# Four-layer image kernel: spectral row transforms moved between the input blocks, a wider layer norm in the attention, and the triangle layer's two outer stages written in 512-column steps

## The chip, the cores and the metric

The kernel runs on one core of one Trainium2 chip. The metric is device time in microseconds (us) for one launch, as the median of several runs. All arithmetic is in float32.

## The reference, cut to what matters

The input `x` has shape 1 x 256 x 256 x 128: 65,536 pixels of 128 channels. Four layers follow, each of the form `x = x + layer(group_norm(x))`.

```python
# layer 0: attention along each image row, 4 heads of 32
zn = layer_norm(z) * ln_scale + ln_bias
q, k, v, g = zn @ Wq, zn @ Wk, zn @ Wv, sigmoid(zn @ Wg)
bias = zn @ Wb                                   # 4 numbers a pixel
o = softmax(q k^T / sqrt(32) + bias) v;  out = (g * o) @ Wo

# layer 1: a recurrence of 16 steps whose coefficients are spectra of 7x7 kernels
A_f = fft2(pad(A_real + 1j * A_imag, 256, 256))  # the same for B
...

# layer 2: triangle
pn = layer_norm(pair)
left, right = sigmoid(pn @ g_in) * (pn @ p_in)   # two halves of 128
out = einsum('bikd,bjkd->bijd', left, right / 256)
out = layer_norm(out) @ p_out
out = sigmoid(pn @ g_out) * out

# layer 3: 3x3 convolution, then a 128 x 128 product
```

The 2-D transforms of the 7 x 7 kernels are computed as two small products: first over the rows (the "spectral row transforms" of the change), later over the columns.

## The kernel before, in words

Activations live in device memory in transposed form, channels on the 128 partitions and pixels along the free axis. `run` calls the stages one after another, and each stage writes an image of 32 MiB that the next one reads.

- `transpose_in` (L137 to L160) reads 64 blocks of 1024 pixels. A block is loaded on SyncE's queue (L146), transposed by eight 128 x 128 TensorE transposes into a PSUM tile `pt` of two banks (L150, pool `p0s` with three buffers), copied out half by VectorE and half by ScalarE (L154, L156), put through two `bn_stats` (L159), and stored to `xT` on GpSimd's queue (L160).
- `spectra` (L532) does the row transforms after that. For each of the two kernels A and B it clears a tile `ka`, fills it with four small loads on SyncE's queue (L545), and for 16 groups of four channels does four matmuls `ph` (L56, 21 rows contracted, 14 output rows, 256 columns) and one strided copy into `H`: on VectorE for A (L555), on ScalarE for B (L553). Each finished half of `H` is stored to `HD`.
- `attention` first sums up the statistics (`group_affine`, the aggregation at L75), makes the weights, and runs a front stage over 64 blocks of 1024 pixels, in two halves of 512. A half calls `layer_norm` (L105 to L118): matmul `zc`, Square on ScalarE to `sq`, matmul `var`, Ln and Exp on ScalarE to `rs`, one VectorE operation to `zn` (L118). Then comes the matmul `pbias` with four output rows, and a VectorE addition to `bi` (L212). `zn` and `bi` are stored on GpSimd's queue (L213, L214). Afterwards `attend_bounded` does the attention, in an order pinned by hand.
- `recurrence` follows, over 64 blocks.
- `triangle` has three stages over the same pixels. The first (L830 to L887) works on 64 blocks of 1024 columns, in an order pinned by hand. For block b it does the three sigmoid gates (`pe`, `pgl`, `pgr`) and the two gated products (`pl`, `pr`), and between them the centring, squares, variance and normalising of block b + 2. Every matmul pair covers 1024 columns, and ScalarE, VectorE operations are 1024 wide. Two table loads of ScalarE stand in each block (L832), around Ln and Exp. The output gates of the first 22 blocks stay in on-chip memory (`kept`); those of the other 42 go through `gateD`. The second stage (L908 to L928) multiplies left and right for each of 128 channels. The third (L940 to L965) takes blocks of 1024 columns: matmuls `zc`, `var`, `py`, in between Square, Ln, Exp on ScalarE and `on`, `y`, `x3`, `bn_stats` on VectorE.
- `convolution` is the last stage.

Where no order is pinned, a scheduler at build time fixes one order for each engine. Every engine then works through its own list in that order and waits, at an instruction, for what that instruction needs; a tile pool with n buffers lets n uses of a tile be under way. In the front stage of the attention and in `transpose_in` the order is the scheduler's; Ln, Exp and table loads are chained in the order of the text (`chain`).

Of the kernel before, what the change touches and what calls it, by code (L numbers as in the profile page):

```python
# [9 lines left out]
F32 = mybir.dt.float32  # L10
# [7 lines left out]
P = 128  # L18
# [12 lines left out]
class Kernel:  # L31
# [105 lines left out]
    def transpose_in(self, xT, stats):  # L137

        nc, tc = self.nc, self.tc
        x = self.i["x"].rearrange("b h w c -> (b h w) c")  # L140
        with ExitStack() as c:
            io = c.enter_context(tc.tile_pool(name="p0", bufs=3))
            ps = c.enter_context(tc.tile_pool(name="p0s", bufs=3, space=PSUM))
            for b in range(NPIX // 1024):
# [15 lines left out]
                nc.gpsimd.dma_start(xT[:, b * 1024:(b + 1) * 1024], xf)  # L160

    def attention(self, xT, x1T, znT, biasD, stats0, stats1):
        nc, tc, I = self.nc, self.tc, self.i
        with ExitStack() as c:
# [31 lines left out]

            with ExitStack() as c1:
                io = c1.enter_context(tc.tile_pool(name="a1", bufs=3))
                work = c1.enter_context(tc.tile_pool(name="a1w", bufs=3))
                ps = c1.enter_context(tc.tile_pool(name="a1s", bufs=2, space=PSUM))  # L200
                self.table(LN_EXP)
                for b in range(NPIX // 1024):
                    xin = io.tile([P, 1024], F32, name="xin")
                    nc.sync.dma_start(xin, xT[:, b * 1024:(b + 1) * 1024])
                    zn = io.tile([P, 1024], F32, name="zn")
                    bi = io.tile([NH, 1024], F32, name="bi")
                    for h in range(2):
                        s = slice(h * 512, (h + 1) * 512)
                        self.layer_norm(zn[:, s], xin[:, s], lc, cb, work, ps, "table")
                        pb = ps.tile([NH, 512], F32, name="pbias")  # L210
                        self.mm(pb, w["b"], zn[:, s])
                        nc.vector.tensor_scalar_add(bi[:, s], pb, wb["b"])  # L212
                    nc.gpsimd.dma_start(znT[:, b * 1024:(b + 1) * 1024], zn)  # L213
                    nc.gpsimd.dma_start(biasD[:, b * 1024:(b + 1) * 1024], bi)  # L214
# [317 lines left out]
    def spectra(self, HD_, name):  # L532

        nc, tc, I = self.nc, self.tc, self.i
        with ExitStack() as c:
            sp = c.enter_context(tc.tile_pool(name=name, bufs=1))
            ps = c.enter_context(tc.tile_pool(name=name + "s", bufs=2, space=PSUM))
            tu = self.load(sp, I["c_rows"], "tu")
            H = sp.tile([46, N, HC], F32, name="H")
            for n, (re, im) in enumerate((("A_real", "A_imag"), ("B_real", "B_imag"))):  # L540
                kr, ki = (I["L1_conv_" + x].rearrange("c p q -> p c q") for x in (re, im))
                ka = sp.tile([3 * KS, HC, 2 * KS], F32, name=f"ka{n}")
                nc.vector.memset(ka, 0.0)
                for p0, q0, src in ((0, 0, kr), (0, KS, ki), (KS, 0, ki), (2 * KS, KS, kr)):
                    nc.sync.dma_start(ka[p0:p0 + KS, :, q0:q0 + KS], src)  # L545
                o = 32 * n
                for c0 in range(0, HC, 4):
                    ph = ps.tile([P, 4, N], F32, name="ph", tag=f"ph{n}")
                    for cc in range(4):
                        self.mm(ph[o:o + 2 * KS, cc, :], ka[:, c0 + cc, :], tu)  # L550
                    dst = H[o:o + 2 * KS, :, c0:c0 + 4].rearrange("q u c -> q c u")
                    if n:
                        nc.scalar.copy(dst, ph[o:o + 2 * KS])  # L553
                    else:
                        nc.vector.tensor_copy(dst, ph[o:o + 2 * KS])  # L555
                nc.sync.dma_start(HD_[n], H[o:o + 2 * KS])

# [240 lines left out]
    def triangle(self, x2T, x3T, leftD, rightD, gateD, prodD, stats2, stats3):  # L798
        nc, tc, I = self.nc, self.tc, self.i
        with ExitStack() as c:  # L800
            wp = c.enter_context(tc.tile_pool(name="tw", bufs=1))
            w, wb = {}, {}
            with tc.tile_pool(name="twp", bufs=2, space=PSUM) as ps0:
# [8 lines left out]
                for nm, m, c0, sc, bb in (("pl", "p", 0, lnw, lnb), ("pr", "p", P, lnw, lnb),  # L812
                                        ("gl", "g", 0, lnw, lnb), ("gr", "g", P, lnw, lnb),
                                        ("e", "e", 0, lnw, lnb), ("o", "o", 0, low, lob)):
                    rw = raw[m][:, c0:c0 + P]
                    pb = ps0.tile([P, 2], F32, name="tpb" + nm, tag="gn")
                    self.mm(pb[:, 0:1], rw, bb)
                    wb[nm] = wp.tile([P, 1], F32, name="twb" + nm)
                    nc.vector.tensor_copy(wb[nm], pb[:, 0:1])
                    w[nm] = wp.tile([P, P], F32, name="tw" + nm)  # L820
                    nc.vector.tensor_scalar_mul(w[nm], rw, sc)


            NB, KEPT = NPIX // 1024, 22
            kept = c.enter_context(tc.tile_pool(name="tk", bufs=1)).tile([P, KEPT, 1024], F32, name="kept")
            with ExitStack() as c1:
                io = c1.enter_context(tc.tile_pool(name="t1", bufs=2))
                work = c1.enter_context(tc.tile_pool(name="t1w", bufs=2))
                ps = c1.enter_context(tc.tile_pool(name="t1s", bufs=3, space=PSUM))
                pin = lambda f: lambda *a, **k: tc.keep_in_program_order(f(*a, **k))  # L830
                mm, act, stt = pin(self.mm), pin(self.act), pin(nc.vector.scalar_tensor_tensor)
                table = lambda n: tc.keep_in_program_order(nc.scalar.preload_act_table_set(n))  # L832
                D = [{} for _ in range(NB)]
                flat = lambda t: t.rearrange("p k n -> p (k n)")

                def product(name, wt, src, **kw):
                    z = ps.tile([P, 2, 512], F32, name=name, **kw)
                    for k in range(2):
                        mm(z[:, k], wt, src[:, k * 512:(k + 1) * 512])
                    return flat(z)  # L840

                def centre(b):
                    if b < NB:
                        xin = io.tile([P, 1024], F32, name="xin")
                        nc.sync.dma_start(xin, x2T[:, b * 1024:(b + 1) * 1024])
                        D[b]["zc"] = product("zc", lc, xin, bufs=1)

                def squares(b):
                    if b < NB:
                        sq = D[b]["sq"] = work.tile([P, 1024], F32, name="sq")  # L850
                        act(sq, D[b]["zc"], AF.Square, bias=cb)

                def variance(b):
                    if b < NB:
                        D[b]["var"] = product("var", self.omat, D[b]["sq"], tag="z")

                def normalise(b):
                    if b < NB:
                        rs = work.tile([P, 1024], F32, name="rs")
                        act(rs, D[b]["var"], AF.Ln, bias=self.eps)  # L860
                        act(rs, rs, AF.Exp, scale=-0.5)
                        zn = D[b]["zn"] = work.tile([P, 1024], F32, name="zn", bufs=3)
                        stt(zn, D[b]["zc"], cb, rs, ALU.add, ALU.mult)

                def gate(b, nm, out):
                    z = product("p" + nm, w[nm], D[b]["zn"], tag="z")
                    act(out, z, AF.Sigmoid, bias=wb[nm])
                    return out

                def gated(b, nm, g, dst):  # L870
                    z = product("p" + nm, w["p" + nm], D[b]["zn"], tag="z")
                    o = io.tile([P, 1024], F32, name="t" + nm)
                    stt(o, z, wb["p" + nm], g, ALU.add, ALU.mult)
                    nc.gpsimd.dma_start(dst[:, b * 1024:(b + 1) * 1024], o)

                table(LN_EXP)
                for b in range(2):
                    centre(b)
                    squares(b)
                    variance(b)  # L880
                    normalise(b)
                table(SIGMOID)
                for b in range(NB):
                    e = kept[:, b] if b < KEPT else io.tile([P, 1024], F32, name="te")
                    gate(b, "e", e)
                    if b >= KEPT:
                        nc.gpsimd.dma_start(gateD[:, b * 1024:(b + 1) * 1024], e)  # L887
                    gl = gate(b, "gl", work.tile([P, 1024], F32, name="sgl"))
                    centre(b + 2)
                    squares(b + 2)  # L890
# [40 lines left out]
            with ExitStack() as c1:  # L931
# [5 lines left out]
                for b in range(NB):  # L937
# [12 lines left out]
                    for k in range(2):  # L950
                        self.mm(zc[:, k], self.cmat, pr[:, k * 512:(k + 1) * 512])
# [249 lines left out]
```

## Time and profile before

| What | us |
|---|---|
| median of three runs | 6563.59 (6561.63 to 6569.74) |
| profiled execution, its own time | 6569.74 |
| its span, first to last instruction | 6567.7 |
| input transposes, to the last `bn_stats` | 0 to 199 |
| spectral row transforms, to the aggregation | 199 to 329 |
| front stage of the attention, with its weights | 329 to 844 |
| attention | 844 to 2293 |
| recurrence | 2293 to 4378 |
| triangle, weights and first stage | 4378 to 5170 |
| triangle, second stage | 5170 to 5560 |
| triangle, third stage | 5560 to 5973 |
| convolution | 5973 to 6568 |

Over the span TensorE is busy 92%, VectorE 63%, ScalarE 57%. The stage limits are read from the first and last instructions of each stage. The profile gives matmuls as instructions: a float32 matmul of the program is two of them, so `pe` with 128 matmuls of 512 columns shows 256. Since matmuls overlap in their pipeline, the duration of one (592 ns for 512 columns) is longer than the distance between two starts; where the text counts TensorE time it uses the distance.

### The profile page before, as it was taken

To read this page: it belongs to the slowest core of one execution; us is meant where nothing else is said; L and a number is where in the kernel's file an instruction comes from. 1 tells how busy PE (TensorE), PEld (TensorE's weight loads), DVE (VectorE), ACT (ScalarE), POOL (GpSimd) and SP (SyncE) were. 2 spreads that over 40 slices of the span, in tenths; PEclk is the share of its full clock that TensorE was granted. 3 is DMA by queue.
4 is the path that set the end of the run, shared out by engine and by line. 5 is a ranking of instruction groups with operands and counts; after the bars stand their busy time and mean duration, and the time that the engine had idled before them with its cause. 6 is when DMAs were issued, how large, how long until landed. Compare 5 with 4: busy or idle time off the path is not lost. (4 is left out here: it accounts for less than half of the span.)

```text
span 6567.7 us, 72931 instructions
## 1 busy us (share of the span) xinstructions
PE 6011.7 (92%) x27637; PEld 2686.6 (41%) x27637; DVE 4161.4 (63%) x5400; ACT 3756.5 (57%) x4945; POOL 367.5 (6%) x720
## 2 busy tenths in 40 slices
PE   5778889999999989999999999979999999887999
PEld 4211145555555423333333333324444587333554
DVE  5333357777777767887878878763333222778775
ACT  1245556666666666666666666657777543444332
POOL 1011100000000000000000000000111111000000
PEclk6599989999999989999999999999999999998999
DMA  9333322222222121111111111113444688895331
GB/s 339 85 135 136 136 76 69 78 69 76 71 74 73 60 60 49 52 49 49 49 49 56 49 49 52 49 48 131 156 174 176 210 271 261 270 336 207 131 134 64
DMA packets 276107, 765.35 MB, mean 117 GB/s; under 512 B 46148, under 2 KB 82265, under 8 KB 273681
## 3 DMA queue, kind: packets, MB, share of 16 engines
q1 hardware_dynamic: 192908, 469.11, 23.4%
q0 software_dynamic: 82848, 291.55, 11.3%
q8 instruction: 222, 3.64, 0.2%
q14 instruction: 129, 1.05, 0.1%
HBM read 433.63 MB, written 326.89 MB: 116 GB/s over the span
## 5 line engine op out<-in xcount | busy, mean ns | idle before, releaser
L327 DVE TENSOR_TENSOR e<-sc,bT 128x1024 f32<-128x1024 f32 x512 | 624.4, 1220 | 159.5 <-PE sc L56 159.5
L50 ACT ACTIVATE e<-e 128x1024 f32<-128x1024 f32 x512 | 538.3, 1051 | 146.2 <-DVE e L327 146.0
L56 PE MATMUL m<-v,U 128*128 128x512 f32 x1152 | 517.5, 595 | 23.3 <-DVE v L1059 23.3
L56 PE MATMUL var<-sq,omat 128*128 128x512 f32 x768 | 388.0, 614 | 140.4 <-ACT sq L50 139.2
L50 ACT ACTIVATE rs<-var,eps 128x512 f32<-128x512 f32 (+1 forms) x256 | 230.6, 901 | 365.9 <-PE var L56 257.5
L50 ACT ACTIVATE dn<-dn 128x256 f32<-128x256 f32 (+1 forms) x640 | 290.3, 454 | 154.0 <-DVE dn L327 145.7
L56 PE MATMUL sc<-tq,tk 32*128 32x256 f32 x4096 | 321.0, 400 | 2.7 <-DVE e L327 2.7
L830 DVE SCALAR_TENSOR_TENSOR tl<-pl,twbpl,sgl 128x1024 f32<-128x1024 f32 x64 | 82.2, 1284 | 359.7 <-ACT sgr L50 336.9
L56 PEld LDWEIGHTS m<-v,U 128*128 128x128 f32 x1152 | 210.4, 191 | 241.5 <-issue 234.3
L212 DVE TENSOR_SCALAR bi<-pbias,wbb 4x512 f32<-4x512 f32 x128 | 94.5, 738 | 316.1 <-PE pbias L56 316.1
L56 PEld LDWEIGHTS var<-sq,omat 128*128 128x128 f32 x768 | 132.7, 189 | 382.1 <-ACT sq L50 273.4
L919 DVE COPY k<-pt 128x256 f32<-128x256 f32 x256 | 96.8, 419 | 285.0 <-PE pt L913 277.0
L56 PE MATMUL nd<-e,tv 128*32 128x256 f32 x4096 | 274.9, 386 | 0.0
L56 PE MATMUL zc<-xin,lc 128*128 128x512 f32 x512 | 269.2, 629 | 4.7 <-DVE zn L830 3.8
L56 PE MATMUL nd<-e,ones 128*32 128x256 f32 x4096 | 268.2, 379 | 0.0
L56 PE MATMUL po<-k,k 128*128 128x256 f32 x1024 | 253.2, 390 | 8.2 <-DVE k L919 0.6
L56 PEld LDWEIGHTS sc<-tq,tk 32*128 32x128 f32 x4096 | 213.9, 184 | 111.8 <-issue 103.7
L56 PE MATMUL zi<-xf,gwi 128*64 128x512 f32 x512 | 188.5, 613 | 67.9 <-DVE q L615 67.9
L50 ACT ACTIVATE sq<-zc,cb 128x512 f32<-128x512 f32 (+1 forms) x192 | 159.3, 829 | 136.8 <-PE zc L56 136.8
L56 PE MATMUL za<-ev,hs 14*128 14x512 f32 x256 | 156.9, 720 | 84.9 <-DVE A L611 79.1
L1079 ACT COPY o<-pt 128x512 f32<-128x512 f32 x128 | 74.6, 584 | 273.4 <-PE pt L1077 263.0
L50 ACT ACTIVATE rs<-rs 128x512 f32<-128x512 f32 (+1 forms) x256 | 216.1, 844 | 7.2
(343 smaller groups left out, 12363.4 us busy)
## 6 DMA issues: line engine op xcount, KB each, us to landing
xin<-x2T SPq DMA_DIRECT2D x128, 512.0 KB
xin<-in_x_dram SPq DMA_DIRECT2D x64, 512.0 KB
xT<-xo POOLq DMA_DIRECT2D x64, 512.0 KB, 7.2
xin<-xT SPq DMA_DIRECT2D x64, 512.0 KB
znT<-zn POOLq DMA_DIRECT2D x64, 512.0 KB, 2.9
zn<-znT SPq DMA_DIRECT2D x64, 512.0 KB
xr<-xT SPq DMA_DIRECT2D x64, 512.0 KB
x1T<-x POOLq DMA_DIRECT2D x64, 512.0 KB, 5.0
```

The lines of the kernel that those rows point to most:

```text
L50: return self.nc.scalar.activation(out, in_, func, bias=bias, scale=scale, **kw)
L56: return self.nc.tensor.matmul(out, lhsT, rhs, start=start, stop=stop)
L212: nc.vector.tensor_scalar_add(bi[:, s], pb, wb["b"])
L327: pin = lambda f: lambda *a, **k: tc.keep_in_program_order(f(*a, **k))
L830: pin = lambda f: lambda *a, **k: tc.keep_in_program_order(f(*a, **k))
L919: nc.vector.tensor_copy(t[:, kc], pt[:, kc].rearrange("k a p -> k p a"))
L1079: nc.scalar.copy(o, pt.rearrange("p g t c -> p g (t c)"))
```

## The change

It has three parts.

1. `spectra` is gone as a stage. `transpose_in` now clears and fills both `ka` tiles first, with the eight small loads on ScalarE's queue, and issues the 32 groups of `ph` between its blocks (in the text after blocks 8 to 55, two groups in every three blocks). All 32 copies to `H` are on ScalarE. `pt` has two PSUM buffers in place of three, because `ph` takes the other half of PSUM.
2. The front stage of the attention takes 32 blocks of 2048 columns. Its Square, Ln, Exp and `zn` work on 1024 columns; the bias of the four chunks of 512 is done by four matmuls with 32 output columns each, that lie side by side in the array's column groups and fill one 128-row tile, with one VectorE addition for all four. `biasD` is stored by four transfers a block.
3. In the triangle, the pinned order, the look-ahead of two blocks and the kept gates are gone. The first stage does a block of 1024 columns in two halves of 512: layer norm of both, then the gates and products of both, with Tanh in place of Sigmoid and a VectorE operation that turns the one into the other. All 64 blocks of gates go through `gateD`. The third stage also works in halves, with the scheduler's order, one more ScalarE operation a half (`y`), and it reads `gateD` for all blocks.

```diff
-    def transpose_in(self, xT, stats):
+    def transpose_in(self, xT, HD_, stats):
...
-            ps = c.enter_context(tc.tile_pool(name="p0s", bufs=3, space=PSUM))
+            ps = c.enter_context(tc.tile_pool(name="p0s", bufs=2, space=PSUM))
+            tu = self.load(sp, I["c_rows"], "tu")
+            H = sp.tile([46, N, HC], F32, name="H")
...
+                for p0, q0, src in ((0, 0, kr), (0, KS, ki), (KS, 0, ki), (2 * KS, KS, kr)):
+                    nc.scalar.dma_start(k[p0:p0 + KS, :, q0:q0 + KS], src)
...
+            def spectrum(g):
+                n, c0 = divmod(4 * g, HC)
+                o = 32 * n
+                ph = ps.tile([P, 4, N], F32, name="ph")
+                for cc in range(4):
+                    self.mm(ph[o:o + 2 * KS, cc, :], ka[n][:, c0 + cc, :], tu)
+                nc.scalar.copy(H[o:o + 2 * KS, :, c0:c0 + 4].rearrange("q u c -> q c u"), ph[o:o + 2 * KS])
+                if c0 + 4 == HC:
+                    nc.sync.dma_start(HD_[n], H[o:o + 2 * KS])
...
+                if 8 <= b < 56:
+                    g = b - 8
+                    if g % 3 < 2:
+                        spectrum(g // 3 * 2 + g % 3)
...
-                for b in range(NPIX // 1024):
-                    xin = io.tile([P, 1024], F32, name="xin")
...
+                for b in range(NPIX // 2048):
+                    zn = io.tile([P, 2048], F32, name="zn")
+                    xin = io.tile([P, 2048], F32, name="xin")
+                    nc.sync.dma_start(xin, xT[:, b * 2048:(b + 1) * 2048])
                     for h in range(2):
-                        s = slice(h * 512, (h + 1) * 512)
-                        self.layer_norm(zn[:, s], xin[:, s], lc, cb, work, ps, "table")
-                        pb = ps.tile([NH, 512], F32, name="pbias")
-                        self.mm(pb, w["b"], zn[:, s])
-                        nc.vector.tensor_scalar_add(bi[:, s], pb, wb["b"])
+                        zc = ps.tile([P, 2, 512], F32, name="zc")
+                        var = ps.tile([P, 2, 512], F32, name="var", bufs=1)
...
+                        for k in range(2):
+                            self.mm(zc[:, k], lc, xin[:, s:s + 512])
+                        self.act(sq, zc, AF.Square, bias=cb)
+                        for k in range(2):
+                            self.mm(var[:, k], self.omat, sq[:, k])
+                        ch(self.act(rs, var, AF.Ln, bias=self.eps))
+                        ch(self.act(rs, rs, AF.Exp, scale=-0.5))
+                        nc.vector.scalar_tensor_tensor(zn[:, h * 1024:(h + 1) * 1024], zc.rearrange("p k n -> p (k n)"), cb,
+                                                       rs.rearrange("p k n -> p (k n)"), ALU.add, ALU.mult)
+                    pb = ps.tile([P, 512], F32, name="pbias")
+                    for k in range(4):
+                        self.mm(pb[32 * k:32 * k + 32], wb32, zn[:, k * 512:(k + 1) * 512])
+                    bi = io.tile([P, 512], F32, name="bi")
+                    nc.vector.tensor_scalar_add(bi, pb, wbb)
...
-            NB, KEPT = NPIX // 1024, 22
...
-                for b in range(NB):
-                    e = kept[:, b] if b < KEPT else io.tile([P, 1024], F32, name="te")
-                    gate(b, "e", e)
...
-                    gl = gate(b, "gl", work.tile([P, 1024], F32, name="sgl"))
-                    centre(b + 2)
-                    squares(b + 2)
-                    gr = gate(b, "gr", work.tile([P, 1024], F32, name="sgr"))
-                    gated(b, "l", gl, leftD)
-                    variance(b + 2)
-                    table(LN_EXP)
-                    normalise(b + 2)
-                    table(SIGMOID)
-                    gated(b, "r", gr, rightD)
+                for b in range(NPIX // 1024):
...
+                    self.table(LN_EXP)
+                    for h in range(2):
+                        s = slice(h * 512, (h + 1) * 512)
+                        self.layer_norm(zn[:, s], xin[:, s], lc, cb, work, ps, "table")
+                    self.table(EXP_TANH)
+                    for h in range(2):
+                        s = slice(h * 512, (h + 1) * 512)
+                        for nm in ("l", "r"):
+                            pg = ps.tile([P, 512], F32, name="pg", tag="pg")
+                            self.mm(pg, w["g" + nm], zn[:, s])
+                            sg = work.tile([P, 512], F32, name="sg")
+                            self.chain("table", self.act(sg, pg, AF.Tanh, bias=wb["g" + nm], scale=0.5))
+                            nc.vector.tensor_scalar(sg, sg, 0.5, 0.5, ALU.mult, ALU.add)
+                            pp = ps.tile([P, 512], F32, name="pp", tag="pp")
+                            self.mm(pp, w["p" + nm], zn[:, s])
+                            nc.vector.scalar_tensor_tensor(outs[nm][:, s], pp, wb["p" + nm], sg, ALU.add, ALU.mult)
+                        pg = ps.tile([P, 512], F32, name="pge", tag="pg")
+                        self.mm(pg, w["e"], zn[:, s])
+                        self.chain("table", self.act(outs["e"][:, s], pg, AF.Tanh, bias=wb["e"], scale=0.5))
+                    for nm, dst in (("l", leftD), ("r", rightD), ("e", gateD)):
+                        nc.gpsimd.dma_start(dst[:, cols], outs[nm])
...
+                    nc.sync.dma_start(ga, gateD[:, cols])
...
+                    for h in range(2):
+                        s = slice(h * 512, (h + 1) * 512)
+                        on = work.tile([P, 512], F32, name="on")
+                        self.layer_norm(on, pr[:, s], self.cmat, self.zero, work, ps, "table")
+                        py = ps.tile([P, 512], F32, name="py")
+                        self.mm(py, w["o"], on)
+                        y = work.tile([P, 512], F32, name="y")
+                        self.act(y, py, AF.Identity, bias=wb["o"], scale=0.5)
+                        nc.vector.scalar_tensor_tensor(y, ga[:, s], 1.0, y, ALU.add, ALU.mult)
+                        nc.vector.tensor_tensor(x3[:, s], y, xin[:, s], ALU.add)
+                        nc.vector.bn_stats(stats3[:, 2 * b + h, :], x3[:, s])
```

`layer_norm`, which the new triangle stages call, is the helper of L105 to L118 described above, here on 512 columns. The weights of the three gates and of the output keep their values; their biases are halved, for the Tanh.

## The prediction

> **What bounds the kernel now.** I first read the busy time of each engine in the five stages that the change touches: time, TensorE (PE), weight loads, VectorE (DVE), ScalarE (ACT), GpSimd, granted TensorE clock, DMA share, GB/s.
>
> ```profile
> 0.00:207.00 207.00, 113.61 (x512) 94.74 (x512) 120.50 (x198) 38.80 (x65) 34.46 (x68) 0.61 0.94 326
> 207.00:317.00 110.00, 107.65 (x256) 34.92 (x256) 29.93 (x16) 28.99 (x16) 0.00 (x0) 0.50 0.08 9
> 346.00:846.00 500.00, 397.58 (x767) 87.28 (x766) 178.96 (x256) 254.31 (x381) 67.72 (x128) 1.00 0.38 133
> 4405.00:5170.00 765.00, 763.47 (x1779) 337.52 (x1777) 239.49 (x191) 585.34 (x509) 89.72 (x169) 1.00 0.43 157
> 5570.00:5960.00 390.00, 343.92 (x747) 134.08 (x748) 305.37 (x311) 192.31 (x187) 33.07 (x62) 1.00 0.87 302
> ```
>
> The transposes are bound by transfers, the row transforms by TensorE at half clock with idle transfers, the triangle's first stage by TensorE without a gap. The attention's front stage and the triangle's third stage fill no engine: there a chain of waits sets the pace. The timeline of the front stage shows that chain (start, duration, engine):
>
> ```profile
> 599.81 1.12 PE L56 MATMUL var<-sq,omat 128*128 128x512 f32 x2 [0.78 <-ACT sq L50]
> 600.86 1.02 PE L56 MATMUL pbias<-zn,wb 128*4 128x512 f32 x2
> 600.97 0.69 ACT L50 ACTIVATE rs<-var,eps 128x512 f32<-128x512 f32 x1 [1.22 <-PE var L56]
> 601.69 0.63 ACT L50 ACTIVATE rs<-rs 128x512 f32<-128x512 f32 x1
> 601.81 1.12 PE L56 MATMUL zc<-xin,lc 128*128 128x512 f32 x2
> 602.59 0.73 DVE L118 SCALAR_TENSOR_TENSOR zn<-zc,cb,rs 128x512 f32<-128x512 f32 x1
> 602.98 0.69 ACT L50 ACTIVATE sq<-zc,cb 128x512 f32<-128x512 f32 x1 [0.66 <-PE zc L56]
> ```
>
> One half is `var` 1.05, `pbias` 0.95, `zc` until ScalarE can read it 1.17, Square 0.69, hand-over 0.05: 3.91 us. From this I take my prices: a matmul of 512 columns that had to wait delays the next by 1.05 and is readable 1.16 after its start; in an unbroken run it costs 0.857 (`pe`, `pgl`, ... start 1.715 apart for two) and is readable after 1.06; hand-overs from ScalarE or VectorE cost 0.03 to 0.05. The third view is ScalarE's timeline in the triangle's first stage:
>
> ```profile
> 4606.75 1.28 ACT L832 ACT_TABLE_LOAD   x1
> 4609.05 1.11 ACT L50 ACTIVATE rs<-var,eps 128x1024 f32<-128x1024 f32 x1 [1.02 <-PE var L56]
> 4610.20 1.06 ACT L50 ACTIVATE rs<-rs 128x1024 f32<-128x1024 f32 x1
> 4611.27 1.28 ACT L832 ACT_TABLE_LOAD   x1
> 4612.57 1.12 ACT L50 ACTIVATE kept<-pe,twbe 128x1024 f32<-128x1024 f32 x1
> ```
>
> Table loads, Ln and Exp of block b + 2 run beside TensorE's work for block b, and cost nothing while TensorE has other matmuls to do.
>
> **What the skill says.** "ScalarE: Activation LUTs", section What ACT_TABLE_LOAD costs, prices a switch at about 1283 ns and a drain of 1380 ns. The trace agrees with the first (1.28) and shows no drain (4611.27 + 1.28, next start 4612.57); I use 1.28. "TensorE: Matmul & The Clock Gate", Part 1, says that activity lifts the half clock. The 21 x 14 matmuls contradict that for thin operands: 110 us without a gap stayed at 0.50. Its Part 3 says that outputs in different column groups run side by side. The trace agrees: in the attention 16 instructions `nd<-e,ones 128*32` of 256 columns start within 0.97 us, where one after the other at 0.213 would be 3.4.
>
> **Part 1, transforms between the blocks.** Removed: the stretch between the transposes' last statistics (199) and the aggregation (329.4), 130 us. Added is the same TensorE work, 128 matmuls at 0.854 (half clock) = 109 us, beside transfers. I read where it stands from the order of the built program: not evenly over the blocks. 88 of the matmuls stand among the first 29 blocks, 40 in a row behind block 29, then 35 blocks follow with none. Transposes at half clock take 1.94 a block, transfers pace a block at about 3.0 (192 us for 64).
> - First 29 blocks: 29 x 1.94 + 88 x 0.854 = 131 us, TensorE-bound (transfers would need 87). Then 40 x 0.854 = 34. With the start at 7 us the matmuls end at 172.
> - From there transfers bind. Three loads are ahead, so 32 loads and 35 stores of 0.524 MB remain, and SyncE's order puts three loads of `xT` (1.05 MB each) for the next stage between them: 38.3 MB at 341 GB/s (67.1 MB in 197 us before) = 112. The second `HD` store, queued on SyncE ahead of further loads, fills the DMA engines for some 6 us (the window 264 to 270 with the first store, 153 GB/s). The last store need not be waited for, -5. Sum 113: statistics end at 286.
> - ScalarE's 32 copies of 1.86 = 59 us lie beside TensorE (3.4 us per group); queued behind a waiting copy are the block copies, which TensorE needs two blocks later, 3.6 us at least, so they do not bind. The eight small loads go out on ScalarE before anything else. Two `pt` buffers suffice for a stream with transforms in it.
> Gain 329.4 - 286 = 43. Bounds: 20 if small loads and block copies hold TensorE up, 105 if mixing lifts the clock so that transfers bind throughout.
>
> **Part 2, front stage.** The built order of a block of 2048 is: `zc` of the first half (2 matmuls), two `pbias` of the block before, one `zc` of the second half, two `var`, one `zc`, two `var`, two `pbias`. ScalarE has Square, Ln, Square, Exp, Ln, Exp. Count from the first `zc`. The two late `pbias` wait for the block before's `zn` and start at 2.2; beside each other they cost 0.95; `zc` 0.86; so `var` starts at 4.04 and is readable at 5.96. Ln 1.11 and Square 1.11 end at 8.2. Second `var` 8.25; Exp of the first half ends at 9.3, `zn` (1.28) at 10.6, so `pbias` starts at 10.7 (`var` + 2.41), +0.95, and the next block starts at 11.65. Before: 4 x 3.91 = 15.64. 32 x 3.99 = 128, less some 3 of a longer start: gain 125. Four `biasD` stores and one `znT` are 5 x 0.53 = 2.7 us on GpSimd's queue per 11.65. Bounds: `pbias` pairs one after the other make it 13.0 (gain 85); 11.2 would be a gain of 140.
>
> **Part 3, first triangle stage.** In the built order nothing of a block crosses the next: TensorE has `zc` x2, `var` x2, ten gate and product matmuls; ScalarE has load, Square x2, Ln, Exp, Ln, Exp, load, Tanh x6. Count from the start of the last gate matmul of the block before. It is readable at 1.06, its Tanh (0.69, as a Square of 512) ends at 1.75; load to 3.06; Squares to 3.77 and 4.46. `var` starts at 3.81 and 4.76, readable at 4.97 and 5.82; Ln, Exp, Ln, Exp to 6.32 and 7.67. `zn` 0.75, so the first gate matmul starts at 7.15. The second load (to 8.97) is hidden behind matmuls. Ten matmuls: 1.05 + 9 x 0.857 after the first start are the next block's; the last gate starts at 7.15 + 1.05 + 8 x 0.857 = 15.05. Before: 14 x 0.857 = 12.0. 64 x 15.05 = 963, against 4388 to 5170 = 782 with its fill: loss 181 to 183. The 1.28 load, the chain Square to `zn`, which the look-ahead had hidden, are what is late now. Writing 22 more gates (11.5 MB) is hidden (DMA share 0.43). Bounds: 120 (13.9 a block) and 225.
>
> **Part 3, third stage.** Order: TensorE `py`, `zc'`, `py`, `var'`, `zc'`, `var'` in halves; ScalarE y, Square, y, Ln, Exp, Square, Ln, Exp. The second `py` needs the second `on`, which is ready at the last `var` + 1.16 + 1.35 (Ln, Exp) + 0.78 + 0.05 = 3.34; `py` starts 0.9 after that `var`, so the second `py` starts at 2.44. `var'` 3.39; y ends at 4.29, Ln and Exp run from 4.45 to 5.8, Square to 6.51, second `var'` 6.55, next block 7.5. 64 x 7.5 = 480 against 410: loss 70. Transfers need 64 x 2.10 MB at 336 GB/s (5800 to 5850) = 399 and stay hidden. Bounds: 15 and 95. The new ScalarE y is in the chain only through its place ahead of Ln.
>
> Setup edits are a few VectorE instructions of 0.15 to 0.3 in gaps: nothing. The second triangle stage, attention, recurrence and convolution keep their text.
>
> **Sum.** -43 - 125 + 182 + 70 = +84 on the profiled execution's own 6569.7 (span 6567.7), which lies 6.1 above the median; on the median 6563.6 it gives about 6648.
>
> **Rivals.**
> - Half clock lifted: busy transposes between transforms, gain 105 in part 1, time 6586. For it: some windows among the transposes had 0.75 to 0.89. Against: the transforms' flat 0.50.
> - Column groups in turn: part 2 gains 85, time 6688. Against: `nd`. For: only two stand together.
> - Third stage at about 6.65 a block: +15, time 6593. For: half-width pieces may overlap better than my chain.
> - Faster than before: TensorE stays the bound of the first triangle stage, 12.0 a block as now, loss nil, time 6466. It decides below 15.05 - 84/64 = 13.74 a block. Against: the order leaves ScalarE's load and Squares behind the last Tanh.
>
> **How the numbers follow.** Forecast 0.63 (own range 6610 to 6690), lifted clock 0.11, groups in turn 0.11, third stage 0.10, faster 0.05. The range 6588 to 6705 leaves out the faster case and the outer parts of the others (15 in 100 in all). About 0.2% (13 us) is what a measurement tells from no change: faster 0.05, the last rival; same 0.03, where the lifted clock and the quicker third stage come together; slower 0.92.
>
> **What would show it.** After: aggregation at about 286, clock near 0.5 up to 172; front stage 11.6 a block; `ACT_TABLE_LOAD` twice in 15 us with TensorE idle before `var` and the first gate; third stage 7.5. A first triangle stage under 13.7 makes the forecast wrong in sign.

## The result and the profile after

The changed kernel takes 6635.68 us (median of four runs, 6630.26 to 6640.89), the kernel before in its four runs 6565.12 (6561.63 to 6569.74). The ratio is 1.0107, 95% interval 1.0089 to 1.0124: 71 us slower, where 84 was forecast. The profiled execution spans 6635.7 us against 6567.7, so the traces differ by 68.0, and the stages of the two traces say where:

| Stage | forecast | traces | what is compared |
|---|---|---|---|
| transposes and transforms | -43 | -52.5 | aggregation starts at 276.9, before at 329.4 |
| front stage | -125 | -125.8 | first `zc` to last `bi`: 377.4, before 503.2 |
| triangle, first stage | +182 | +180.7 | first `zc` to first `po` of the next stage: 971.3, before 790.6 |
| triangle, third stage | +70 | +69.2 | end of the last `po` to first `xp` of the convolution: 511.7, before 442.5 |
| everything else | 0 | -3.6 | attention, recurrence and weights -1.8, second triangle stage -2.1, convolution +0.3 |

In the triangle's first stage a block takes 14.98 us, before 12.0, which would make 191; 10 us of that are not lost, mostly because the stage before had the longer head: its look-ahead has to be filled first, and its first gate starts 17.0 us after its first `zc`. The 12.0 is the distance of the first gate's matmuls in the kernel before, 63 blocks from the first to the last:

```profile
L56 PE MATMUL pe<-zn,twe x256: 592/592/593, 4405.8 to 5161.2; 128*128 128x512 f32 x128
```

The busy times of the changed kernel by stage (time, TensorE, weight loads, VectorE, ScalarE, GpSimd, granted clock, DMA share, GB/s):

```profile
0.00:160.00 160.00, 150.46 (x498) 73.87 (x499) 57.69 (x94) 75.93 (x62) 15.74 (x33) 0.64 0.64 209
160.00:277.00 117.00, 59.17 (x274) 48.83 (x272) 66.81 (x117) 20.52 (x35) 18.66 (x35) 0.60 0.96 336
287.00:664.00 377.00, 310.82 (x768) 99.68 (x768) 106.35 (x103) 203.44 (x192) 79.79 (x156) 0.99 0.47 170
4210.00:5170.00 960.00, 804.84 (x1791) 329.88 (x1790) 391.76 (x640) 670.00 (x896) 110.74 (x191) 1.00 0.38 138
5560.00:6035.00 475.00, 365.11 (x768) 135.31 (x766) 343.58 (x512) 323.82 (x512) 33.80 (x64) 1.00 0.84 279
```

The first two rows are the stage that was to overlap: TensorE is nearly full for 160 us with the transfers at 0.64, then the transfers are full with TensorE at half. The two limits still follow each other more than they overlap. In the fourth row TensorE, full before, is busy 805 of 960: 155 us of gaps. Nearly all of them are two waits: 87.3 us before the first gate matmul `pg`, for `zn`, and 66.9 before `var`, for the Square.

**Transposes and transforms.** TensorE's timeline (start, duration, of a run of alike instructions; x8 of `ph` are four matmuls, x8 of `pt` one block):

```profile
86.77 4.44 PE L56 MATMUL ph<-tu,ka 21*14 21x256 f32 x10
...
94.74 1.89 PE L56 MATMUL ph<-tu,ka 21*14 21x256 f32 x8
96.56 1.09 PE L175 MATMUL pt<-ident,xin 128*128 128x128 f32 x8
...
123.63 26.63 PE L56 MATMUL ph<-tu,ka 21*14 21x256 f32 x62
...
157.87 5.29 PE L175 MATMUL pt<-ident,xin 128*128 128x128 f32 x24
173.56 1.94 PE L175 MATMUL pt<-ident,xin 128*128 128x128 f32 x8 [10.40 <-DMA xin<-in_x_dram]
```

Among the blocks some transforms and transposes go at twice the pace of others: eight `ph` in 1.89 beside ten in 4.44, eight `pt` in 1.09 beside 1.94. So the mixed phase ended at 123.6 and not at 138, and the 40 matmuls in a row (80 instructions, of which that line has the first 62), all at the slow pace (34 us), at 157.9 and not at 172. Then the three blocks already loaded are transposed at once, and TensorE waits 10.4 us for the next: the second `HD` store, issued at 159.9, went ahead of the loads on SyncE's queue, and little else moves until some 172. Two windows of this stage, with the store and later:

```profile
160.00:170.00 10.00, 3.16 (x16) 2.71 (x14) 5.55 (x9) 1.76 (x3) 1.60 (x3) 0.67 1.01 141
190.00:200.00 10.00, 6.20 (x26) 4.71 (x24) 4.97 (x9) 1.76 (x3) 1.60 (x3) 0.50 1.02 372
```

The DMA share is full in both (1.01 and 1.02), but 141 GB/s are moved with the store and 372 without. From 157.9 to the aggregation it is 119 us, where 113 was forecast. The 14 us gained before and the 6 lost here leave the 9 us by which this gain is larger than the forecast.

**Front stage.** The lines of the chain in the timeline, from the first `var` of a block to the `zc` behind its late `pbias`:

```profile
501.80 1.88 PE L56 MATMUL var<-sq,omat 128*128 128x512 f32 x4
...
503.71 1.11 ACT L50 ACTIVATE rs<-var,eps 128x1024 f32<-128x1024 f32 x1 [3.08 <-PE var L56]
...
504.73 1.11 ACT L50 ACTIVATE sq<-zc,cb 128x1024 f32<-128x1024 f32 x1
...
505.89 1.98 PE L56 MATMUL var<-sq,omat 128*128 128x512 f32 x4 [1.35 <-ACT sq L50]
...
508.15 1.05 PE L56 MATMUL pbias<-zn,wb 128*32 128x512 f32 x4 [0.28 <-DVE zn L257]
...
509.13 1.98 PE L56 MATMUL zc<-xin,lc 128*128 128x512 f32 x4
```

This is the forecast chain link for link: `var`, Ln, Square, second `var`, with Exp and `zn` beside it, then `pbias`. The next block's `var` starts at 513.43, so a block takes 11.63. Two matmuls `pbias` (x4) delay `zc` by 0.98 us, hardly more than one had cost before (0.95): the two column groups run side by side.

**Triangle, first stage.** ScalarE's timeline over the end of one block and the head of the next:

```profile
4599.81 0.69 ACT L50 ACTIVATE te<-pge,twbe 128x512 f32<-128x512 f32 x1 [1.03 <-PE pge L56]
4600.51 1.28 ACT L53 ACT_TABLE_LOAD   x1
4601.81 1.27 ACT L50 ACTIVATE sq<-zc,cb 128x512 f32<-128x512 f32 x2
...
4606.32 1.28 ACT L53 ACT_TABLE_LOAD   x1
...
4614.79 0.69 ACT L50 ACTIVATE te<-pge,twbe 128x512 f32<-128x512 f32 x1 [1.03 <-PE pge L56]
4615.49 1.28 ACT L53 ACT_TABLE_LOAD   x1
```

and TensorE's over the same block:

```profile
4599.61 1.88 PE L56 MATMUL zc<-xin,lc 128*128 128x512 f32 x4
4602.55 1.98 PE L56 MATMUL var<-sq,omat 128*128 128x512 f32 x4 [1.06 <-ACT sq L50]
4605.90 1.13 PE L56 MATMUL pg<-zn,twgl 128*128 128x512 f32 x2 [1.37 <-DVE zn L118]
```

From load to load it is 14.98. `zc` is long done when the first Square starts, so TensorE's 1.06 ahead of `var` is the table load's doing; its 1.37 ahead of `pg` is the normalisation. The second load runs for 1.28 from 4606.32 while TensorE has gate and product matmuls to do. Lines like `[1.06 <-ACT sq L50]` name only the last link: the Square itself waited for the load that stands in front of it on its own engine, and carries no wait.

**Triangle, third stage.** Matmuls and ScalarE's lines of one block in the timeline:

```profile
5700.28 1.12 PE L56 MATMUL py<-on,two 128*128 128x512 f32 x2 [0.51 <-DVE on L118]
...
5701.25 1.02 PE L56 MATMUL var<-sq,omat 128*128 128x512 f32 x2
5701.45 0.69 ACT L50 ACTIVATE y<-py,twbo 128x512 f32<-128x512 f32 x1 [0.85 <-PE py L56]
...
5702.31 0.69 ACT L50 ACTIVATE rs<-var,eps 128x512 f32<-128x512 f32 x1 [0.17 <-PE var L56]
...
5703.56 0.67 ACT L50 ACTIVATE sq<-zc,zero 128x512 f32<-128x512 f32 x1
...
5704.29 1.12 PE L56 MATMUL var<-sq,omat 128*128 128x512 f32 x2 [1.16 <-ACT sq L50]
...
5707.64 1.13 PE L56 MATMUL py<-on,two 128*128 128x512 f32 x2 [0.51 <-DVE on L118]
```

A block takes 5707.64 - 5700.28 = 7.36 (7.5 forecast). The second `var` of a block waits for a Square that stands behind Ln and Exp of the first: ScalarE is handed half-width pieces one after the other, and TensorE waits 1.16 for this Square and 0.51 for `on`.

### The profile page after: what moved, and what is told of

The parts are those of the page before. It is cut to its first block, busy times and chain, and to the rows that moved or that the text cites. A ratio compares the mean times of both kernels' runs of the same rounds, so it can differ in the third digit from the quotient of the medians.

```text
span 6635.7 us, 74161 instructions
## 1 busy us (share of the span) xinstructions
PE 5947.8 (90%) x27637; PEld 2676.1 (40%) x27637; DVE 4241.6 (64%) x5871; ACT 3937.6 (59%) x5471; POOL 402.8 (6%) x774
## 3 DMA queue, kind: packets, MB, share of 16 engines
q14 instruction: 139, 1.14, 0.1%
## 5 line engine op out<-in xcount | busy, mean ns | idle before, releaser
L50 ACT ACTIVATE e<-e 128x1024 f32<-128x1024 f32 x512 | 538.1, 1051 | 146.1 <-DVE e L380 145.9
L50 ACT ACTIVATE rs<-var,eps 128x512 f32<-128x512 f32 (+1 forms) x320 | 246.3, 770 | 260.7 <-PE var L56 260.7
L50 ACT ACTIVATE dn<-dn 128x256 f32<-128x256 f32 (+1 forms) x640 | 290.3, 454 | 154.1 <-DVE dn L380 145.9
L118 DVE SCALAR_TENSOR_TENSOR zn<-zc,cb,rs 128x512 f32<-128x512 f32 x128 | 96.1, 751 | 352.9 <-ACT rs L50 352.9
L50 ACT ACTIVATE rs<-rs 128x512 f32<-128x512 f32 (+1 forms) x320 | 229.0, 715 | 9.2
L257 DVE SCALAR_TENSOR_TENSOR zn<-zc,cb,rs 128x1024 f32<-128x1024 f32 x64 | 82.2, 1284 | 233.6 <-ACT rs L50 233.6
```

Source lines behind the costliest of these rows:

```text
L50: return self.nc.scalar.activation(out, in_, func, bias=bias, scale=scale, **kw)
L118: nc.vector.scalar_tensor_tensor(out, zc, cb, rs, ALU.add, ALU.mult)
L257: nc.vector.scalar_tensor_tensor(zn[:, h * 1024:(h + 1) * 1024], zc.rearrange("p k n -> p (k n)"), cb, rs.rearrange("p k n -> p (k n)"), A ...
```

## The experiments

Each kernel was timed beside the kernel before on the same chip; ratios are to it. Theory: the four terms of the forecast are independent; the losses come from chains that no other work covers (the first table load and the normalisation in the first stage, narrow pieces in the third), not from traffic, width as such, or gates that are no longer kept. The rivals stand with each run.

**Do the parts add up?** The triangle of before was put back into the changed kernel; only `transpose_in` and the front stage are new.

```diff
-                for b in range(NPIX // 1024):
-                    self.table(LN_EXP)
...
+            NB, KEPT = NPIX // 1024, 22
...
+                    gl = gate(b, "gl", work.tile([P, 1024], F32, name="sgl"))
+                    centre(b + 2)
+                    squares(b + 2)
...
```

> The kernel before with the transforms between the blocks and the new front stage, but with its own triangle (1024-wide first stage with look-ahead, 22 gates kept, 1024-wide third stage). If the four parts add up, as the traces of the two kernels say, this is 52 + 126 = 178 us faster than before: about 6387. The rival: the early parts and the triangle are coupled (through loads of weights, buffers or the clock), so that some of the gain is given back: then 6420 or more.

Measured: 6391.7, ratio 0.9737 (0.9721 to 0.9753), 177 less than before. Then the first part alone, with the front stage of before as well:

```diff
-                for b in range(NPIX // 2048):
+                for b in range(NPIX // 1024):
...
-                    for k in range(4):
-                        self.mm(pb[32 * k:32 * k + 32], wb32, zn[:, k * 512:(k + 1) * 512])
+                        pb = ps.tile([NH, 512], F32, name="pbias")
+                        self.mm(pb, w["b"], zn[:, s])
...
```

> Only the transforms are moved between the transposed blocks. My theory: the gain is 52 (from the traces; 43 was forecast), about 6512, aggregation at about 277. The rival of a clock that is lifted in general by mixing: the same place with a gain of 105, 6460.

Measured: 6518.6, ratio 0.9926 (0.9909 to 0.9942), 50.5 less; aggregation at 276.5. By difference the front stage is 127 (126 in the traces), and the triangle 6635.7 - 6391.7 = 244 (248 in the traces, forecast 252). So the parts add up, and the slower kernel contained a kernel 2.6% faster than before.

**Which of the two loads costs?** In the changed kernel the Tanh of the first stage became Exp, which computes something else but takes as long (0.69), so that one load ahead of the stage's loop serves all.

```diff
+                self.table(LN_EXP)
...
-                    self.table(LN_EXP)
...
-                    self.table(EXP_TANH)
...
-                            self.chain("table", self.act(sg, pg, AF.Tanh, bias=wb["g" + nm], scale=0.5))
+                            self.chain("table", self.act(sg, pg, AF.Exp, bias=wb["g" + nm], scale=0.5))
```

> The changed kernel with Exp in place of Tanh in the triangle's first stage, so that one table load at the head of the stage is enough (the gates are then exponentials, which changes the computation). My theory: of the two loads per block only the first stands in the chain, the second lies beside matmuls: 15.0 to 13.7 a block, 64 x 1.28 = 82 us less than the changed kernel, about 6554. If both loads were in the chain: 164 less, about 6472. If TensorE were the bound: no gain, 6636.

Measured: 6566.5, ratio 0.9996 (0.9987 to 1.0005), against 1.0107 for the changed kernel: 69 us less by the medians, 73 by the ratios. ScalarE's timeline of this run:

```profile
4612.44 0.69 ACT L50 ACTIVATE te<-pge,twbe 128x512 f32<-128x512 f32 x1 [1.03 <-PE pge L56]
4613.30 0.69 ACT L50 ACTIVATE sq<-zc,cb 128x512 f32<-128x512 f32 x1 [0.17 <-PE zc L56]
...
4626.28 0.69 ACT L50 ACTIVATE te<-pge,twbe 128x512 f32<-128x512 f32 x1 [1.03 <-PE pge L56]
```

The block's last gate comes again after 4626.28 - 4612.44 = 13.84; with two loads it was 14.98. Both loads of a block are gone, and less than one is gained; TensorE's wait before `var` is gone with them, its 1.37 before the first `pg` is still there. So the first load stands in the chain and the second is hidden, as forecast. It gives back 1.14 and not its 1.28, because the Square now waits for what the load had covered, 0.17 for `zc`. In the traces 72.0 of the stage's 180.7 are gone and 108.7 remain: the normalisation itself, uncovered.

**Was it the gates that are no longer kept?** The kernel before with none kept:

```diff
-            NB, KEPT = NPIX // 1024, 22
+            NB, KEPT = NPIX // 1024, 0
```

> The kernel before, with no gates kept on the chip: all 64 blocks of output gates are written out and read back, as in the changed kernel. My theory: the extra 22 stores and 22 loads of 0.524 MB are hidden in both stages (DMA share 0.43 and 0.87 before): first stage 12.0 a block, third stage 6.25 a block or a little more, total 6565 within 10. The rival: the traffic is what the third stage lost, 64 x 2.10 MB bind there, up to 70 more, 6635.

Measured: 6570.4, ratio 1.0001 (0.9992 to 1.0010). Its busy times in the windows of the first and third stage:

```profile
4405.00:5170.00 765.00, 759.67 (x1770) 336.07 (x1768) 239.01 (x191) 582.04 (x507) 101.49 (x192) 1.00 0.48 173
5570.00:5960.00 390.00, 342.63 (x744) 133.12 (x742) 306.42 (x312) 191.11 (x186) 32.96 (x62) 1.00 0.91 327
```

The DMA share rises (0.43 to 0.48, 0.87 to 0.91), the stages keep their pace. The extra traffic is hidden, in the third stage with 9% to spare. So this rival falls.

**Is the third stage's loss its width?** The changed kernel with the third stage of before, `ga` read for all blocks:

```diff
-                    for h in range(2):
...
-                        self.layer_norm(on, pr[:, s], self.cmat, self.zero, work, ps, "table")
...
+                    self.act(sq, flat(zc), AF.Square)
...
+                    ch(self.act(rs, flat(var), AF.Ln, bias=self.eps))
+                    ch(self.act(rs, rs, AF.Exp, scale=-0.5))
+                    nc.vector.tensor_tensor(on, flat(zc), rs, ALU.mult)
...
+                    nc.vector.scalar_tensor_tensor(y, flat(py), wb["o"], ga, ALU.add, ALU.mult)
```

> The changed kernel with the 1024-wide third stage of the kernel before (the whole output gate is read back as Tanh; its turning into a sigmoid, two more operations, is left out). My theory: the loss of 69 in this stage is the chain of half-width pieces, and goes: about 6567. The rival: the 22 more gate loads, or the gates that are no longer kept, cost part of it: 6590 or more.

Measured: 6573.2, ratio 1.0014 (1.0007 to 1.0021): 61 (by the ratios, give or take 13) to 63 (by the medians) less than the changed kernel. The third stage has its old pace. The operation `on` before and in this run:

```profile
L957 DVE TENSOR_TENSOR on<-zc,rs x64: 1224/1225/1226, 5571.1 to 5963.2; 128x1024 f32<-128x1024 f32 x64
L938 DVE TENSOR_TENSOR on<-zc,rs x64: 1224/1225/1226, 5571.1 to 5963.4; 128x1024 f32<-128x1024 f32 x64
```

With 63 distances that is 6.22 and 6.23 a block. The edit takes away the extra operation `y` on ScalarE as well as the halves, and the two were not tried apart. In the changed kernel's timeline no link of the chain waits for `y`: it is done at 5702.14, and the Ln behind it still waits 0.17 for `var`. So the width is the likely cause.

The 5 us that this run misses lie behind the last block: from the last `on` to the first `xp` it takes 37.4, before 32.8. The kernel before with no gates kept has 35.7 there, and the five other experiments with the wide third stage, which keep 22 gates, 31.6 to 33.0. So the rival is met by some 3 to 5 us behind the stage, while nothing is lost in a block.

**Is the first stage's loss its width?** The kernel before with every ScalarE and VectorE operation of that stage in two halves, its order and look-ahead kept:

```diff
-                mm, act, stt = pin(self.mm), pin(self.act), pin(nc.vector.scalar_tensor_tensor)
+                mm = pin(self.mm)
+                def act(out, z, *a, **k):
+                    for h in range(2):
+                        s = slice(h * 512, (h + 1) * 512)
+                        tc.keep_in_program_order(self.act(out[:, s], z[:, s], *a, **k))
...
```

> The kernel before with every ScalarE and VectorE operation of the triangle's first stage cut into two of 512 columns, in the same pinned look-ahead order. My theory: the missing look-ahead is what the changed kernel loses there, not its width; TensorE stays the bound at 12.0 a block, or nearly (ScalarE then has 12 pieces of 0.63 to 0.69 and two loads of 1.28, 10.7 of 12.0): 6565 to 6585. The rival: narrow pieces by themselves bring about 15 a block: 6565 + 180 = 6745.

Measured: 6564.9, ratio 0.9999 (0.9990 to 1.0008). Its window over the stage:

```profile
4405.00:5170.00 765.00, 764.22 (x1776) 338.41 (x1776) 260.59 (x378) 629.56 (x889) 88.89 (x168) 1.00 0.43 157
```

ScalarE has 889 instructions for 509 and 44 us more to do, and TensorE is still busy 764 of 765. Narrow pieces cost nothing where another block's matmuls cover them. With width and kept gates excluded and one load measured, what is left for the first stage's loss is that nothing of block b + 2 runs beside block b. The changed kernel with a look-ahead put into it was not tried.

**Width or packing in the front stage?** The changed kernel with the 512-wide layer norm, its packed bias kept:

```diff
-                    for h in range(2):
-                        zc = ps.tile([P, 2, 512], F32, name="zc")
...
+                    for h in range(4):
+                        s = slice(h * 512, (h + 1) * 512)
+                        self.layer_norm(zn[:, s], xin[:, s], lc, cb, work, ps, "table")
```

> The changed kernel with 512-wide layer norm in the front stage, the packed pair bias kept. My theory: width gives most of the 126. By the order built here two of the four pair bias matmuls of a block still stand between a var and the next zc (3.91 a half), two lie under a Square (Ln, Exp, Square then set 3.26): 14.3 a block of 2048, 42 of the 126 kept, so 84 more than the changed kernel, 6720. The rival, packing alone: 11.6 a block, 6636. The other end, packing gives nothing: 15.6 a block, 6762.

Measured: 6718.4, ratio 1.0236 (1.0219 to 1.0253), 83 more than the changed kernel by the medians, 85 by the ratios. TensorE's timeline shows both kinds of halves:

```profile
503.82 1.13 PE L56 MATMUL var<-sq,omat 128*128 128x512 f32 x2 [0.78 <-ACT sq L50]
504.87 1.05 PE L56 MATMUL pbias<-zn,wb 128*32 128x512 f32 x2
505.85 1.12 PE L56 MATMUL zc<-xin,lc 128*128 128x512 f32 x2
507.75 1.13 PE L56 MATMUL var<-sq,omat 128*128 128x512 f32 x2 [0.78 <-ACT sq L50]
508.71 1.02 PE L56 MATMUL zc<-xin,lc 128*128 128x512 f32 x2
509.67 1.04 PE L56 MATMUL pbias<-zn,wb 128*32 128x512 f32 x2
510.89 1.12 PE L56 MATMUL var<-sq,omat 128*128 128x512 f32 x2 [0.18 <-ACT sq L50]
```

With `pbias` between `var` and `zc` a half takes 507.75 - 503.82 = 3.93; with `pbias` behind `zc`, beside the Square, 510.89 - 507.75 = 3.14. Two of each are 14.14 a block of 2048, against 15.64 before and 11.63 in the changed kernel. From the first `zc` to the last `bi` this run takes 456.7, against 503.2 and 377.4. So of the 126, width is worth 79; the other 46 are had with half-width pieces too, and by these lines they come from where `pbias` stands: here no two stand together, so nothing runs side by side.

**Can the first part overlap better?** The two parts of the first experiment, with four groups of transforms to every seven blocks from block 2 on, in a pinned order:

```diff
-                if 8 <= b < 56:
-                    g = b - 8
-                    if g % 3 < 2:
-                        spectrum(g // 3 * 2 + g % 3)
+                g, k = divmod(b - 2, 7)
+                if 0 <= g < 8 and k % 2 == 0:
+                    spectrum(4 * g + k // 2)
```

> The early parts with the triangle of before (about 6391), the transforms now spread evenly, four groups of four to seven blocks, in a pinned order. My theory: in the changed kernel 40 transforms in a row left the transfers idle for some 35 us; spread, each seven blocks cost TensorE 16 x 0.854 + 7 x 1.06 to 1.94 = 21 to 27 us beside 21 us of transfers, so aggregation comes at about 235, 42 earlier: 6350. If TensorE's half clock held everywhere: 250 and 6365. If the order of the stores or the second HD store were the cause, nothing: 6391.

Measured: 6356.2, ratio 0.9681 (0.9665 to 0.9697), 35 less than without the spread; aggregation at 247.8. The row of 40 was a cause, then, but not all of my theory holds: the time lies between my figure (6350) and the half-clock one (6365), and the aggregation is nearer to the half-clock one (250) than to mine (235). For long stretches, such as 40 to 68, every group of `ph` took 3.59 and every block of `pt` 1.8 to 2.0. So the slow transforms were the next thing to make cheaper:

```diff
-                for cc in range(4):
-                    pin(self.mm(ph[o:o + 2 * KS, cc, :], ka[n][:, c0 + cc, :], tu))
+                for cc in (0, 2, 1, 3):
+                    rs = slice(32 * (cc // 2), 32 * (cc // 2) + 3 * KS)
+                    pin(self.mm(ph[o:o + 2 * KS, cc, :], ka[n][rs, c0 + cc, :], tu[rs]))
```

> The evenly spread version, with the 21-row transforms of every second channel on rows 32 to 52 of the array instead of rows 0 to 20 (operands loaded twice, 16 small loads instead of 8), so that two matmuls can run side by side. My theory: after the even spread TensorE, at half clock in the transforms, still takes part of the pace (128 x 0.854 = 109 us); two side by side halve that, transfers bind alone (67 MB at 341 GB/s, 197 us), aggregation some 25 earlier than in the evenly spread version, about 6330. The rival: transfers already bind there, or matmuls in different row groups run one after the other: no change, 6356.

Measured: 6338.6, ratio 0.9654 (0.9638 to 0.9671), 18 less than the even spread; aggregation at 225.4, 22 earlier. TensorE's timeline of the evenly spread kernel

```profile
111.50 3.59 PE L56 MATMUL ph<-tu,ka 21*14 21x256 f32 x8
115.02 1.97 PE L177 MATMUL pt<-ident,xin 128*128 128x128 f32 x8
```

and of the one with two row groups:

```profile
105.45 1.89 PE L56 MATMUL ph<-tu,ka 21*14 21x256 f32 x8
107.27 1.97 PE L181 MATMUL pt<-ident,xin 128*128 128x128 f32 x8
...
114.29 1.04 PE L56 MATMUL ph<-tu,ka 21*14 21x256 f32 x8
115.82 1.06 PE L181 MATMUL pt<-ident,xin 128*128 128x128 f32 x8 [0.49 <-DMA xin<-in_x_dram]
127.49 1.94 PE L181 MATMUL pt<-ident,xin 128*128 128x128 f32 x8 [10.61 <-DMA xin<-in_x_dram]
```

Next to transposes at the same slow pace (1.97), a group takes 1.89 in place of 3.59, and 1.04 next to fast ones: two matmuls side by side. TensorE now waits for `xin`, so transfers set the pace, with a DMA share of 0.97 from 40 to 225. The last line is the first `HD` store (issued at 109.6) holding up the loads for ten microseconds, as in the changed kernel; the second does it again, for 9.0. Another 13.0 us at the start were not foreseen: the 16 small loads keep ScalarE until 24.4, and TensorE waits for its first block copies (1.9 in the evenly spread kernel, with 8 small loads). The Trainium skill states the row groups in "TensorE: Matmul & The Clock Gate", section Why this matters for your kernels, with a factor of 3.07 for four of them at once; with two the trace shows 1.9. This is the fastest version of the study: the forecast's two gains, the first of them doubled, without its two losses.

## Why the prediction was right

- **Sum and sign.** +84 was forecast, +71 measured, +68 between the traces. The largest part of the difference is the first term.
- **Transforms, -43: right in kind, too small by 9.5.** The step "29 x 1.94 + 88 x 0.854 = 131 us" took the half clock for all of the mixed phase; it ended 14 us early, since part of it ran at the full pace. The step that gave the second store "some 6 us" was too low: with the 10.4 us for which TensorE waited, the rest came to 119 for 113. The 6 was the length of the window that was read; its DMA share of 1.36 says that the transfers which start in it last beyond it, and by the trace's packet records the first store runs from 265.7 to 276.0. Two errors of opposite sign, -14 and +6, are in this term. The lifted clock, my rival of 105, is thus true in part; it is not steady, though: the same part ended its transforms at 157.9 in the changed kernel, at 161.4 in the first experiment and at 164.3 in the second, with the aggregation at 276.9, 278.5 and 276.5. The larger share of the gap to 105 was the row of 40 and the cost of the slow transforms, of which the last two experiments removed the one and halved the other: 329.4 to 225.4 is 104.
- **Front stage, -125: right.** 11.63 a block for 11.65. "Column groups in turn" falls by the 0.98 for a pair. That width gives 79 and the place of `pbias` the rest was not in the forecast's working, and came out of an experiment.
- **Triangle, first stage, +182: right.** 14.98 for 15.05; the first load counts (69 to 73 measured for 82), the second is hidden. The rival that TensorE stays the bound falls: it would need less than 13.74 a block, and even with both loads gone the changed order has 13.84.
- **Triangle, third stage, +70: right, the closeness in part luck.** 7.36 for 7.5 a block, 61 to 63 given back by the old stage. The pace was put 0.14 too high, 9 us in 64 blocks, and "480 against 410" set bare blocks against a stage with head and tail (64 x 6.22 is 398), which hid as much. The quicker third stage, 6.65 a block, falls. That its transfers stay hidden was shown at 0.91 of the DMA engines.
- **Edits costed at nothing** (setup, five transfers a block on GpSimd's queue, the extra gate traffic) cost nothing that the runs show.

What stays open: what decides when the clock goes up among transposes and transforms, whether a look-ahead alone would win back the rest of the first stage, and width against `y` in the third.

## What to carry to other kernels

Narrow or wide pieces, and a table load more or less, are decided by one question: has TensorE matmuls of another block to do meanwhile? Half-width pieces cost nothing under the look-ahead of the first stage, and 61 to 79 us in the two stages where a chain of waits sets the pace; of two equal table loads one cost its time and the other none. Work that is meant to fill the gaps of a transfer-bound stage must be spread over the whole stage in the built order, and must be looked for there, since the text of the program had it spread, and the built program had nearly a third of it in one row.

## What the runs showed of the hardware

- **Clock.** The 21 x 14 matmuls, at half pace for 110 us when alone, ran at both paces among transposes (eight in 3.59 or 1.89), and so did the transposes (eight in 1.97 or 1.06). "TensorE: Matmul & The Clock Gate", Part 4, says that the full clock does not engage for transposes; here it does, at times, in this mixture and also where nothing but transposes runs (before, from 60 to 125: eight in 1.94 or 1.06). In the first 80 us of the evenly spread kernel the clock column shows 1.00 while eight `ph` take 3.59; the durations, not the column, are to be believed there.
- **A transfer with few rows.** `HD` is stored from 14 partitions, 0.92 MB. TensorE waited 10.40 us (changed kernel) and 10.61 us (row groups) for the loads queued behind such a store. By the trace's packet records the changed kernel's second store is 14 packets of 65,536 bytes, half of them 10.6 us long or longer, from 160.7 to 171.9; the packets of the block loads, 4,096 bytes, take 0.16 us each. In the kernel before, where nothing else is moved beside the first store, half of its packets take 10.0 us or longer too. So such a packet takes some 10 us whether others wait or not; that it holds one of the 16 DMA engines all the while fits the share of 1.01, but is not shown, and why it is so slow is not shown either. A window counts a packet in full where it starts, so the low GB/s after the start of such a store are not idle engines.
